# Two-part transformer kernel on one core: a shorter setup ahead of the first block, the rest of the setup as a job of its own, and loads in another order

## The chip, the core and the metric

The kernel runs on one core of a Trainium2 chip. Its engines each have an instruction queue that they work through in order: TensorE (PE, with its weight loads shown as PEld), VectorE (DVE), ScalarE (ACT), GpSimd (POOL) and SyncE (SP), which here only issues DMA transfers. ScalarE and GpSimd issue some transfers too; those of GpSimd stand in the profile as a software queue. The metric is the device time of one execution in microseconds (us); lower is better. The profile's times count from the start of the span.

## The reference

The tokens x are 2 batches of 2048 rows of 256 numbers, all in float32. A vector c of each batch gives six rows of modulation, and two networks follow, the first of 3 layers of linear attention (16 heads), the second of 2 layers of windowed attention. Cut to what matters here:

```python
mod = silu(c) @ wmod                 # 6 rows of 256 per batch: shift, 1 + scale, gate, twice
h = layernorm(x) * (1 + scale_1) + shift_1
for l in range(3):                   # linear attention with exponential features of omega
    q, k, v = h @ Wq[l] + bq[l], h @ Wk[l] + bk[l], h @ Wv[l] + bv[l]
    a = causal_linear_attention(exp_features(q, omega[l]), exp_features(k, omega[l]), v)
    h = layernorm(h + a @ Wo[l] + bo[l]) * ln1_g[l] + ln1_b[l]
    h = layernorm(h + relu(h @ W1[l] + bf1[l]) @ W2[l] + bf2[l]) * ln2_g[l] + ln2_b[l]
x = x + gate_1 * h
h = layernorm(x) * (1 + scale_2) + shift_2
# two layers of windowed attention and a gated MLP on h, then x + gate_2 * (their output)
```

## The kernel before

**Setup.** `vec` holds c and all small parameters as columns, `cst` the identity and masks, `wmod` the modulation weights. A silu of c (`sg`) is multiplied by all six parts of `wmod` in 24 products of two columns each (`pm`, L300), which become `mod`. Parameters that are added or multiplied along the free dimension are wanted as rows, the same in every partition (`brow`, 18 rows: R_G1, R_B1, R_G2, R_B2 for the layers, R_G0, R_B0 for the first norm, R_GE, R_BE for the end). `spread` makes them on the engines: VectorE copies two columns out to 512 wide (`wide`, L279), TensorE turns them in four transposes (`rowtp`, L287), ScalarE copies them into `brow` (L288); nine such rounds. `omt` (L330 to L337) is omega laid out for the heads, from `om_rep`, which GpSimd loads in eight pieces.

**Loads.** SyncE's queue holds, in this order: `vec`, `cst`, one half of `wmod`, the tokens of the first two blocks, the weights of all three layers, the tokens of the third and fourth block. ScalarE issues the other half of `wmod` and the first layer's `Wq`. GpSimd issues `bvb` and `om_rep`.

**Blocks.** The first part works on 16 blocks (b, n) of 256 tokens, n in order and both batches in turn. `favor_block` norms the tokens (`normed`: statistics L354, `dn` L361), turns them (`turned`: `ntp` L371, evicted into `h` L375), makes the residual rows on GpSimd (`scaled`: `res`, L384 and L385, which read `brow`), and runs three layers. A layer (`favor_layer`) is: projections `pq` (L414, evicted by VectorE into `xs` L425, squared by ScalarE L426) and `pv` (L430), features `pu` (L453), running sum `z` (VectorE L475, then GpSimd's copy `zl` L484 and product L485), transposes `tk`, scores `sc` (L500), `su`, denominators `den` (L548, which read `z`), `nd`, output `po` (L602), norm, and the MLP with `pf` (L624), `fr` (L632) and `acc` (L635).

**Order.** `planned` takes the blocks as generators and keeps four of them live; each step says how much TensorE time it takes and how long its result needs, and the block that is ready first goes next. TensorE's queue in the first part is exactly that order. The other engines and SyncE get their order from a list scheduler. At the start all four live blocks are normed and turned before the first `pq`.

**Seam.** The last block stores `hm` to DRAM (L690), the second part loads it as `s` (L724), and the weights `w2` (L198) are loaded about there too. The second part has an order written out by hand, which the change doesn't touch.

Of the kernel before, what the change touches and what calls it, by code (L numbers as in the profile page):

```python
# [39 lines left out]
def block_kernel(ctx: ExitStack, tc: tile.TileContext, t: dict, out: bass.AP):  # L40
# [19 lines left out]
    nc.sync.dma_start(cst, t["consts"])  # L60
# [11 lines left out]
    mhalf = const.tile([P, 16], F32, name="mhalf")  # L72
    nc.gpsimd.memset(mhalf, -0.5)
    mod = const.tile([P, 6, KT, B], F32, name="mod")
    omt = const.tile([P, LA, 2, 4, 2, 8], F32, name="omt")
    bvb = const.tile([P, LA, D], F32, name="bvb")
    nc.gpsimd.dma_start(bvb, t["bv"].partition_broadcast(P))
# [134 lines left out]
    with ExitStack() as c1:  # L212
        wp = c1.enter_context(tc.tile_pool(name="wA", bufs=1))
        psum = c1.enter_context(tc.tile_pool(name="psA", bufs=1, space=PSUM))
        brow = wp.tile([P, NROW, D], F32, name="brow")
        hp = c1.enter_context(tc.tile_pool(name="hA", bufs=3))
        work = c1.enter_context(tc.tile_pool(name="workA", bufs=2))

# [10 lines left out]
        with tc.tile_pool(name="pro", bufs=1) as pro:  # L229
            wmod = pro.tile([P, KT, 6 * D], F32, name="wmod")  # L230
            for kt in range(KT):
                (nc.scalar if kt else nc.sync).dma_start(wmod[:, kt, :], t["wmod"][kt * P : (kt + 1) * P, :])
            early = {b: load_x(b, 0) for b in range(B)}
            om_rep = pro.tile([P, LA, 8], F32, name="om_rep")
            for h in range(8):
                nc.gpsimd.dma_start(om_rep[16 * h : 16 * h + 16], t["omega"].rearrange("l d m -> d l m"))
            W = {}
            for l in range(LA):
                pool = shared if l < 2 else wp
                wa = pool.tile([P, ROOM], F32, tag=f"wa{l}", name=f"wa{l}")  # L240
                wb = pool.tile([P, ROOM], F32, tag=f"wb{l}", name=f"wb{l}")
                for room, at, name, kts, width in (
                    (wa, KT * DFF, "Wq", KT, D),
                    (wa, KT * DFF + KT * D, "Wk", KT, D),
                    (wb, NF * D, "Wv", KT, D),
                    (wb, NF * D + KT * D, "Wo", KT, D),
                    (wa, 0, "W1", KT, DFF),
                    (wb, 0, "W2", NF, D),
                ):
                    w = room[:, at : at + kts * width].rearrange("p (k n) -> p k n", k=kts)  # L250
                    (nc.scalar if (name, l) == ("Wq", 0) else nc.sync).dma_start(
                        w, t[name][l].rearrange("(k p) n -> p k n", p=P)
                    )
                    W[name, l] = w

            cv = vec[:, V_C : V_C + KT * B]
            sg = pro.tile([P, KT * B], F32, name="sg")
            nc.scalar.activation(sg, cv, AF.Exp, scale=-1.0)
            nc.vector.tensor_scalar(sg, sg, 1.0, None, ALU.add)
            nc.vector.reciprocal(sg, sg)  # L260
            nc.vector.tensor_tensor(sg, sg, cv, ALU.mult)

            cols = pro.tile([P, NROW, KT], F32, name="cols")

            def col(i, *parts):
                op = parts[2] if len(parts) > 2 else ALU.add
                if len(parts) == 1:
                    nc.vector.tensor_copy(cols[:, i, :], parts[0])
                else:
                    nc.vector.tensor_tensor(cols[:, i, :], parts[0], parts[1], op)  # L270

            def va(l, name):
                o = V_A + l * VA_N + VA[name]
                return vec[:, o : o + KT]

            def spread(lo, hi):
                for i in range(lo, hi, 2):
                    wide = pro.tile([P, 2 * KT, P], F32, tag="wide", name="wide", bufs=2)
                    nc.vector.tensor_copy(  # L279
                        wide,  # L280
                        cols[:, i : i + 2, :].rearrange("p a k -> p (a k)").unsqueeze(2).to_broadcast(
                            [P, 2 * KT, P]
                        ),
                    )
                    tp = mm_tile("rowtp").rearrange("p (a c) -> p a c", c=P)
                    for k in range(2 * KT):
                        nc.tensor.transpose(tp[:, k, :], wide[:, k, :], ident)  # L287
                    nc.scalar.copy(brow[:, i : i + 2, :].rearrange("p a (k c) -> p (a k) c", c=P), tp)  # L288

            for l in range(LA):  # L290
                col(R_G1 + l, va(l, "g1"))
                col(R_B1 + l, va(l, "b1"), va(l, "bf2"))
            for l in range(LA - 1):
                col(R_G2 + l, va(l, "g2"))
                col(R_B2 + l, va(l, "b2"), va(l + 1, "bo"))
            spread(0, R_G0)
            pm = mm_tile("pm")
            for m in range(6 * KT):
                for kt in range(KT):
                    nc.tensor.matmul(  # L300
                        pm[:, m * B : (m + 1) * B],
                        wmod[:, kt, m * P : (m + 1) * P],
                        sg[:, kt * B : (kt + 1) * B],
                        start=(kt == 0),
                        stop=(kt == KT - 1),
                    )
            nc.vector.tensor_copy(mod.rearrange("p a k b -> p (a k b)"), pm[:, : 6 * KT * B])
            for i in (1, 4):
                nc.vector.tensor_scalar(mod[:, i], mod[:, i], 1.0, None, ALU.add)
            for i in (2, 5):  # L310
                sgn = pro.tile([P, KT, B], F32, name=f"sgn{i}")
                nc.vector.tensor_scalar(sgn, mod[:, i], 0.0, 2.0, ALU.is_ge, ALU.mult)
                nc.vector.tensor_scalar(sgn, sgn, -1.0, None, ALU.add)
                neg = pro.tile([P, KT, B], F32, name=f"neg{i}")
                nc.vector.tensor_scalar(neg, mod[:, i], -1.0, None, ALU.mult)
                nc.vector.tensor_tensor(neg, neg, mod[:, i], ALU.max)
                nc.vector.tensor_scalar(neg, neg, 0.25, None, ALU.max)
                nc.vector.tensor_tensor(mod[:, i], sgn, neg, ALU.mult)
            for b in range(B):
                col(R_G0 + b, mod[:, 1, :, b])  # L320
                col(R_B0 + b, mod[:, 0, :, b], va(0, "bo"))
                col(R_GE + b, va(LA - 1, "g2"), mod[:, 2, :, b], ALU.mult)
                col(R_BE + b, va(LA - 1, "b2"), mod[:, 2, :, b], ALU.mult)
            spread(R_G0, NROW)


            for hf in range(2):
                own, other = slice(64 * hf, 64 * hf + 64), slice(64 - 64 * hf, 128 - 64 * hf)
                for l in range(LA):
                    nc.vector.tensor_tensor(  # L330
                        omt[own, l, hf].rearrange("p h s m -> p (h s) m"),
                        om_rep[own, l, :].unsqueeze(1).to_broadcast([64, 8, 8]),
                        hm2[own, 8 * hf : 8 * hf + 8].unsqueeze(2).to_broadcast([64, 8, 8]),
                        ALU.mult,
                    )
                    nc.vector.tensor_scalar(omt[own, l, hf], omt[own, l, hf], 0.5, None, ALU.mult)
                    nc.vector.tensor_scalar(  # L337
                        omt[other, l, hf].rearrange("p h s m -> p (h s m)"),
                        nhalf[other, 64 - 64 * hf : 128 - 64 * hf],
                        0.25,  # L340
                        None,
                        ALU.mult,
                    )

        rp = c1.enter_context(tc.tile_pool(name="rA", bufs=2))
        fp = c1.enter_context(tc.tile_pool(name="featA", bufs=2))
        sp = c1.enter_context(tc.tile_pool(name="smallA", bufs=2))
# [45 lines left out]
        nc.vector.tensor_reduce(par, hmask.rearrange("p (i q) -> p q i", q=2), AX.X, ALU.add)  # L393
# [5 lines left out]
        turn = [0]  # L399

        def favor_layer(b, n, l, h, hres):
# [45 lines left out]
            yield 5.2, 0.6, "attention"  # L447
            feat = []
# [171 lines left out]
            for f in range(NF + 1):  # L620
                if f < NF:
# [9 lines left out]
                    fr[f] = fp.tile([P, TA], F32, tag="fr", name="fr", bufs=3)  # L631
# [37 lines left out]
        def favor_block(b, n):  # L669
            dn = normed(early.pop(b) if n == 0 else load_x(b, n))  # L670
            yield 0.0, 4.0
            h = hp.tile([P, KT, TA], F32, tag="h", name="h0")
            turned(dn, h, lambda k: mod[:, 1, k, b : b + 1], lambda k: mod[:, 0, k, b : b + 1])
            hres = scaled(dn, R_G0 + b, R_B0 + b)
# [18 lines left out]
        with tc.manual_schedule(engines={mybir.EngineType.PE}):  # L693
            planned([favor_block(b, n) for n in range(S // TA) for b in range(B)], 4)
# [632 lines left out]
```

## Time and profile before

| | us |
|---|---|
| median of 3 runs | 3002.98 (3001.48 to 3004.59) |
| profiled execution | 3000.0 |
| its span | 2998.2 |
| PE busy | 2914.3 (97%) |
| DVE, ACT, POOL busy | 1686.0, 1344.5, 1065.1 |
| first `pq` on TensorE | 46.14 |
| mean granted clock | 0.992 |

The first part ends near 1590, the second takes the rest. The page's busy times are sums over the span; what the start costs is seen only in the stretches and in the chain of waits of the first microseconds.

### The profile page before, as it was taken

How to read it: one execution, taken by the hardware profiler on the slowest of the kernel's cores; microseconds unless marked ns; L12 is line 12 of the kernel's file. 1: busy time of each engine (PE TensorE's matmuls, PEld its weight loads, DVE VectorE, ACT ScalarE, POOL GpSimd, SP SyncE). 2: the span in 40 equal slices, each digit the busy share in tenths (PEclk: the TensorE clock that was granted, in tenths of full speed). 3: DMA queues.
4: the chain of work that ended last, by engine and by line, in shares of the span. 5: the costliest groups of instructions: out<-in, count | busy, mean ns of one | idle time of the engine just before them, and what ended most of it. 6: DMA issues, size and time to landing. Idle time of an engine off the chain costs nothing.

```text
span 2998.2 us, 49213 instructions
## 1 busy us (share of the span) xinstructions
PE 2914.3 (97%) x19356; PEld 2132.3 (71%) x19356; DVE 1686.0 (56%) x4194; ACT 1344.5 (45%) x3269; POOL 1065.1 (36%) x937
## 2 busy tenths in 40 slices
PE   6999999999999999999996999999999999999999
PEld 5888888888888888888873777776444777776444
DVE  5555565555565555655543777774224777775222
ACT  2333343334343334434333676665113766766211
POOL 2222233222332223322233666663002666664000
PEclk9999999999999999999997999999999999999999
DMA  5000010000100000001012000001000000000011
GB/s 184 1 1 1 1 36 22 1 1 1 36 22 1 1 1 29 29 1 43 15 42 77 1 1 1 1 1 58 0 0 10 20 1 1 2 1 8 28 43 35
DMA packets 37399, 57.10 MB, mean 19 GB/s; under 512 B 3720, under 2 KB 28720, under 8 KB 36656
## 3 DMA queue, kind: packets, MB, share of 16 engines
q1 hardware_dynamic: 36288, 52.37, 5.3%
q8 instruction: 153, 2.51, 0.3%
q0 software_dynamic: 464, 0.54, 0.1%
q10 hardware_dynamic: 416, 1.05, 0.1%
q14 instruction: 78, 0.64, 0.1%
HBM read 41.37 MB, written 12.58 MB: 18 GB/s over the span
## 4 chain that ended last, share of the span: by engine, by line
PE 88%; DVE 4%; ACT 3%; POOL 2%; DMA 1%; issue 1%; SPq 1%; DVEq 0%; ACTq 0%; POOLq 0%
PE acc L635 11%; PE pf L624 10%; PE pqkv L790 10%; PE pg L1135 5%; PE pq L414 5%; PE acc L1173 5%; PE pa L1135 4%; PE av L979 4%; PE sim L886 3%; PE ptp L953 3%; PE po L998 3%; PE sc L500 3%; PE nd L572 3%; PE pu L453 3%; PE pv L430 3%; PE po L602 3%
## 5 line engine op out<-in xcount | busy, mean ns | idle before, releaser
L635 PE MATMUL acc<-wb,fr 128*128 128x256 f32 x1536 | 397.3, 381 | 5.4 <-ACT fr L632 5.1
L624 PE MATMUL pf<-h,wa 128*128 128x256 f32 x1536 | 400.2, 384 | 1.1 <-ACT h L375 0.7
L632 ACT ACTIVATE fr<-pf,vec 128x256 f32<-128x256 f32 x384 | 180.6, 471 | 425.8 <-PE pf L624 425.0
L790 PE MATMUL pqkv<-wqkv,s 128*128 128x512 f32 x768 | 358.0, 602 | 8.3 <-issue 8.3
L506 DVE TENSOR_TENSOR att<-sc,cst 128x512 f32<-128x512 f32 x384 | 238.3, 683 | 157.6 <-PE sc L500 157.6
L635 PEld LDWEIGHTS acc<-wb,fr 128*128 128x128 f32 x1536 | 287.8, 190 | 52.0 <-ACT fr L632 8.6
L384 POOL TENSOR_TENSOR res<-dn,brow 128x512 f32<-128x512 f32 x112 | 144.7, 1292 | 485.2 <-DVE dn L361 473.5
L624 PEld LDWEIGHTS pf<-h,wa 128*128 128x128 f32 x1536 | 275.8, 190 | 55.7 <-issue 19.5
L941 POOL TENSOR_TENSOR pm<-pm,sum 128x1024 f32<-128x1024 f32 (+1 forms) x128 | 235.7, 1842 | 178.9 <-DVE sum L936 178.9
L926 ACT ACTIVATE pm<-pm,mx 128x256 f32<-128x256 f32 (+1 forms) x512 | 249.4, 489 | 58.9 <-DVE mx L918 58.7
L790 PEld LDWEIGHTS pqkv<-wqkv,s 128*128 128x128 f32 x768 | 138.0, 193 | 135.9 <-issue 134.0
L832 POOL TENSOR_TENSOR rot<-raw,rsn_wo 128x512 f32<-128x512 f32 x128 | 160.5, 1275 | 183.5 <-ACT raw L813 183.5
L1144 DVE SCALAR_TENSOR_TENSOR ge<-pa,vec,ge 128x512 f32<-128x512 f32 x80 | 60.1, 751 | 281.9 <-PE pa L1135 230.6
L1143 ACT ACTIVATE ge<-pg,vec 128x512 f32<-128x512 f32 x96 | 65.8, 686 | 314.9 <-PE pg L1135 314.9
L426 ACT ACTIVATE xs<-xs 64x512 f32<-64x512 f32 x192 | 120.6, 628 | 152.3 <-DVE xs L425 142.8
L1135 PE MATMUL pg<-s,w 128*128 128x512 f32 (+1 forms) x384 | 182.2, 597 | 0.0
L414 PE MATMUL pq<-h,wa 128*128 128x256 f32 x768 | 175.4, 382 | 0.0
L425 DVE TENSOR_TENSOR xs<-pq,vec 64x512 f32<-64x512 f32 x192 | 132.2, 688 | 76.5 <-PE pq L414 72.7
L1173 PE MATMUL acc<-ge,w 128*128 128x512 f32 (+1 forms) x384 | 168.8, 600 | 0.0
L414 PEld LDWEIGHTS pq<-h,wa 128*128 128x128 f32 x768 | 146.1, 191 | 21.1 <-issue 1.4
L854 POOL TENSOR_TENSOR qk<-qk,rot 128x1024 f32<-128x1024 f32 x64 | 151.5, 2367 | 0.5
L1135 PE MATMUL pa<-s,w 128*128 128x512 f32 x320 | 150.4, 592 | 0.0
(163 smaller groups left out, 5361.8 us busy)
## 6 DMA issues: line engine op xcount, KB each, us to landing
xin<-in_x_dram SPq DMA_DIRECT2D x32, 256.0 KB, 2.8
x<-res SPq DMA_DIRECT2D x16, 256.0 KB, 2.1
h<-hm SPq DMA_DIRECT2D x16, 256.0 KB, 2.4
s<-h SPq DMA_DIRECT2D x16, 256.0 KB, 5.4
xl<-x SPq DMA_DIRECT2D x8, 512.0 KB, 4.2
out_dram<-res SPq DMA_DIRECT2D x8, 512.0 KB, 3.2
w<-in_w_dram SPq DMA_DIRECT2D x6, 640.0 KB, 4.0
wa<-in_W_dram SPq DMA_DIRECT2D x3, 1024.0 KB, 8.9
```

The source lines that it names most:

```text
L414: nc.tensor.matmul(pq[:, g, :], W[wn, l][:, kt, g * P : (g + 1) * P], h[:, kt, :], start=(kt == 0), stop=(kt == KT - 1),)
L506: nc.vector.tensor_tensor(am, scs[i].rearrange("p g q c -> p (g q) c"), caus.unsqueeze(1).to_broadcast([P, 2 * KT, P]), ALU.mult,)
L624: nc.tensor.matmul(pf, W["W1", l][:, kt, f * P : (f + 1) * P], h1[:, kt, :], start=(kt == 0), stop=(kt == KT - 1),)
L632: nc.scalar.activation(fr[f], pf, AF.Relu, bias=v("bf1", f))
L635: nc.tensor.matmul(acc[:, c, :], fr[f - 1][:, c * P : (c + 1) * P], W["W2", l][:, f - 1, :], start=(f == 1 and c == 0), stop=(f == NF), sk ...
L790: nc.tensor.matmul(pq, s[:, kt * TB + c * P : kt * TB + (c + 1) * P], wqkv[:, kt, i * INNER : (i + 1) * INNER], start=(kt == 0), stop=(kt ...
L832: nc.gpsimd.tensor_tensor(rot[:, :, :, lo : lo + 32], got["raw"][:, :, :, hi : hi + 32], rsn[:, ti, :, lo : lo + 32].unsqueeze(2).to_broad ...
L854: nc.gpsimd.tensor_tensor(got["qk"], got["qk"], got["rot"], ALU.add)
L926: nc.scalar.activation(pm[:, hd, :], pm[:, hd, :], AF.Exp, bias=of("mx", hg)[:, hd : hd + 1], accum_out=of("sum", hg)[:, hd : hd + 1],)
L941: nc.gpsimd.tensor_tensor(pm, pm, of("sum", hg).unsqueeze(2).to_broadcast([P, 4, kw]), ALU.mult)
L1135: nc.tensor.matmul(pt[:m, :], w1[:, kt, off : off + m], hb[:, kt * TB : (kt + 1) * TB], start=(kt == 0), stop=(kt == KT - 1),)
L1173: nc.tensor.matmul(acc[m], w2[rs_, f, m * P : (m + 1) * P], g[rs_, :], start=(f == 0), stop=(f == NFH - 1),)
```

## The change

It does five things. (1) A new `first_norm`, in a fixed order on TensorE, VectorE and ScalarE, does what the first block needs: `sg`, the first two of six parts of `mod` (8 products), the first block's norm and turning, the columns, the rows R_G0 and R_B0 and the layer rows, and the first layer's `omt`. (2) The other four parts of `mod`, the other layers' `omt`, the last four rows (R_GE, R_BE) and the loads of the third layer's weights become a job, `rest_of_setup`, which `planned` gets as the second of its live jobs; the fourth block enters when that job is done. (3) `spread` makes rows by DMA: one transpose of the columns, one copy, a store to DRAM, and a load of it into all partitions, both issued by GpSimd. (4) The loads are put in another order: the first third of `wmod` alone on ScalarE, then `Wq` and `Wv`; on SyncE the identity first and the rest of `cst` after the tokens of the first two blocks; the third block's tokens after the first layer's `Wk` and `Wo`; `om_rep` ahead of `bvb`. The third layer's weights take the memory of `wmod` and of the setup's small tiles, so they wait for both. (5) The pools are opened in another order, `fr` moves to another pool, and the first two blocks' `res` rows are made one step later.

By the instruction lists, SyncE's order is now: `vec`, identity, tokens (0,0) and (1,0), rest of `cst`, `Wk`, `Wo`, tokens (0,1), `W1`, rest of `wmod`, `W2`, six weights of layer 1, tokens (1,1), two residual loads, six weights of layer 2. TensorE's: 8 products, 4 transposes, 2 row transposes, `pq` and `pv` of the first block, 8 transposes, `pu`, 4 products, `tk`, `sc`, `su`, 8 products, `sc`, `den`, 4 products, `nd`, `pq` of the second block. GpSimd's: the small loads, the clearing of `vp`, two stores and two loads of rows, four operations on `res`, `zl`, `z`. After the first 200 matmuls TensorE's order is that of before. At the seam, `w2` is now loaded among the loads of `s` and not ahead of the last store of `hm`.

```diff
-    nc.sync.dma_start(cst, t["consts"])
+    nc.sync.dma_start(cst[:, :P], t["consts"][:, :P])
...
+        wmod = wp.tile([P, ROOM], F32, tag="wa2", name="wmod").rearrange("p (k n) -> p k n", k=KT)
+        stage = wp.tile([P, ROOM], F32, tag="wb2", name="stage")
+        nc.scalar.dma_start(wmod[:, :, : 2 * D], wmod_in[:, :, : 2 * D])
+        early = {(b, 0): load_x(b, 0) for b in range(B)}
+        nc.sync.dma_start(cst[:, P:], t["consts"][:, P:])
...
+        load_weights(0, "Wq", "Wk", "Wv", "Wo")
+        early[0, 1] = load_x(0, 1)
+        load_weights(0, "W1")
+        nc.sync.dma_start(wmod[:, :, 2 * D :], wmod_in[:, :, 2 * D :])
+        load_weights(0, "W2")
+        load_weights(1, "Wq", "Wk", "Wv", "Wo", "W1", "W2")
...
+        def spread(lo, hi):
+            n = (hi - lo) * KT
+            tp = mm_tile("rowtp")[:n, :P]
+            nc.tensor.transpose(tp, cols[:, lo:hi, :].rearrange("p a k -> p (a k)"), ident)
+            turned_ = turned_cols.pop()[:n]
+            nc.scalar.copy(turned_, tp)
+            nc.gpsimd.dma_start(rows_out[lo * KT : hi * KT], turned_)
+            nc.gpsimd.dma_start(
+                brow[:, lo:hi, :].rearrange("p a d -> p (a d)"),
+                rows_out[lo * KT : hi * KT].rearrange("a c -> (a c)").partition_broadcast(P),
+            )
...
+        def first_norm(normed, turned):
+            with tc.manual_schedule(
+                engines={getattr(mybir.EngineType, e) for e in ("PE", "DVE", "Activation")}
+            ):
...
+                condition(0, 2, pm)
...
+                dn = normed(early.pop((0, 0)))
+                conditioned(0, 2, pm)
+                turned(dn, h, lambda k: mod[:, 1, k, 0:1], lambda k: mod[:, 0, k, 0:1])
...
+                spread(R_G0, R_GE)
+                spread(0, R_G0)
+                omega_rows(0)
...
+        def rest_of_setup():
+            yield 0.0, 8.0, "mlp"
+            pm = psum.tile([P, NCA * D], F32, tag="acc", name="pm2", bufs=1)
+            for i in range(2, 6):
+                condition(i, i + 1, pm)
+                yield 1.7, 0.0, "mlp"
+            conditioned(2, 6, pm)
...
+            spread(R_GE, NROW)
+            load_weights(2, "Wq", "Wk", "Wv", "Wo", "W1", "W2")
+            yield 0.2, 0.0
...
-                    fr[f] = fp.tile([P, TA], F32, tag="fr", name="fr", bufs=3)
+                    fr[f] = work.tile([P, TA], F32, tag="fr", name="fr", bufs=3)
...
-            planned([favor_block(b, n) for n in range(S // TA) for b in range(B)], 4)
+            blocks = [favor_block(b, n) for n in range(S // TA) for b in range(B)]
+            with tc.issue_after(last_first):
+                planned(blocks[:1] + [rest_of_setup()] + blocks[1:], 4)
```

## The prediction

> **What bounds the kernel now.** First the table of stretches (start:end and length in us, then busy us and instructions of PE, PEld, DVE, ACT and POOL, granted clock, DMA share, GB/s):
>
> ```profile
> 10.00:20.00 10.00, 8.63 (x42) 8.18 (x41) 2.95 (x16) 2.34 (x4) 0.14 (x1) 1.00 1.08 363
> 30.00:40.00 10.00, 2.39 (x12) 1.64 (x10) 3.78 (x8) 3.45 (x8) 6.84 (x7) 0.73 0.96 327
> 40.00:46.00 6.00, 2.26 (x8) 1.42 (x9) 4.73 (x11) 2.02 (x6) 4.32 (x4) 0.50 0.17 45
> 200.00:300.00 100.00, 100.00 (x745) 82.74 (x745) 54.17 (x114) 38.94 (x82) 26.50 (x26) 1.00 0.00 1
> ```
>
> After the start, TensorE is full: 99 us or so in each 100 up to about 1500. Work taken off VectorE, ScalarE or GpSimd there buys nothing; a later or earlier start moves the end one for one. Until 38 us the DMA engines are full at 350 to 400 GB/s, and TensorE does only setup. So I looked at who lets it start. The chain of waits over the first 120 us (start, us, what):
>
> ```profile
> 26.99 12.37 DMA xin<-in_x_dram
> ...
> 43.37 2.03 DVE dn L361 x2
> 45.40 0.04 issue
> 45.44 0.90 PE ntp L371 x3
> 46.34 4.50 PE pq L414 x16
> ...
> 64.48 3.65 PE pq L414 x16
> ```
>
> The first projection (pq) of the first block starts at 46.3. Its own tokens came long before, but TensorE's order puts the transposes of all four live blocks ahead of it, and the last two blocks' tokens are queued on SyncE behind the weights of three layers. Everything in front of 46.3 is start-up; the second block's pq, at 64.48, is my mark: from there TensorE's order is the same in both kernels, but for four transposes and one small transpose.
>
> The timeline of the start gives the prices (start, us, engine, line, what):
>
> ```profile
> 14.18 10.24 PE L300 MATMUL pm<-sg,wmod 128*128 128x2 f32 x48
> ...
> 30.56 0.94 PE L371 MATMUL ntp<-cst,dn 128*128 128x128 f32 x4
> ...
> 32.80 1.25 POOL L384 TENSOR_TENSOR res<-dn,brow 128x512 f32<-128x512 f32 x1
> ...
> 56.93 1.27 POOL L485 TENSOR_TENSOR z<-ft,z 128x512 f32<-128x512 f32 x1
> ...
> 60.68 1.13 PE L548 MATMUL den<-z,cst 128*128 128x256 f32 x4
> ```
>
> and the DMA issues of the first 60 us (KB each, median us to landing):
>
> ```profile
> xin<-in_x_dram SPq DMA_DIRECT2D x7, 256.0 KB, 6.5
> wmod<-in_wmod_dram ACTq DMA_DIRECT2D x1, 768.0 KB, 4.5
> bvb<-in_bv_dram POOLq DMA_DIRECT2D x1, 384.0 KB, 8.0
> om_rep<-in_omega_dram POOLq DMA_DIRECT2D x8, 1.5 KB, 7.6
> ```
>
> **The change, part by part.**
>
> *Start of the first pq.* TensorE now does 8 of the 24 conditioning products, four transposes of the first block, two small transposes, then pq. Two inputs race. (1) The first third of wmod, 512 KB, goes first on ScalarE's queue, where 768 KB landed 4.5 us after 0.77, so about 5.3; sg needs vec (landed at 4.09) and is done by then. 8 products are 16 instructions at 10.24/48 = 0.213: 3.4 us, to 8.7 (at the row's longest single duration, 0.35: 10.9). (2) The first tokens are third on SyncE, behind 57 and 64 KB, issued near 1.7; with the median of 6.5 they land at 8.2 (bounds 2.7 and 10.1 from the same issues: 4.4 and 11.8). From tokens to normed tokens the trace shows 39.38 to 42.55, 3.2 us, less where GpSimd is quiet: 11.2. Then transposes 0.9 and two evictions into h 1.0 (after the mod of path 1): 13.1. The tokens' queue is much shorter than it was, so I take 12.5, bounds 10.5 and 16.5. Wq and Wk are the second transfer of their queue and the sixth; Wq landed at 11.44 even beside both halves of wmod.
>
> *From pq to my mark.* Before, 64.48 - 46.34 = 18.1, with a cold start in it (first pq 4.50 for 16 against 3.65). The same chain follows now, also cold: 18.1.
>
> *Added in that stretch.* VectorE in its fixed order does omega_rows(0) and par before the other blocks' statistics and before the first xs. It waits for eight tiny GpSimd loads; issued from 0.8, 0.6 apart, with 7.6 to land, the last is there at about 12.7. The work behind that up to the first xs (omega's last operations and par 0.6, four statistics at 0.4, one dn pair 0.8, smalls) is some 3.8 us, so xs is at 16.5 instead of 15.5, and one more dn pair lies among the four xs: 2 us, bounds 0.5 and 6. Their eight transposes on TensorE (0.11 each warm, 0.2 cold) fall into that wait.
>
> The other 16 conditioning products, 32 instructions, stand between the steps of the first block. No row shows them warm; transposes halve from 0.21 to 0.11 later in the trace, so 3.4 to 6.8 us. They cover two waits that the chain shows: 0.7 for the exponential before tk, and 1.5 in the second group of sc (2.60 for 16 against 1.08). Without this cover they'd cost all 3.4. Net 1.2 to 4.6; I take 2, nearer the warm end as pq has warmed the clock.
>
> *The rows by DMA.* Out go 36 transposes, 9 evictions (0.59) and 9 wide copies, none of it in front of anything that matters once the start moves. In come, on GpSimd's in-order queue, a small store to DRAM, a load of 512 KB broadcast from it (R_G0 and R_B0), and a second pair of 1.3 MB. Behind them on that queue: four res operations (the second and third blocks' scaled rows), which wait for the 512 KB; behind these zl and z of the first block; and for z waits den on TensorE, with all of its order behind. Price: eviction of the rows done at 13.0; store lands after 5.6 to 7.6 (om_rep), say 6.5: 19.5; broadcast 8.0 (bvb, 384 KB; by size 10.7): 27.5; four res of 1.27: 32.6; zl and z 1.5: 34.1. den is due at 12.5 + 14.4 (60.75 - 46.34) + 2 (VectorE) + 0.4 (the products ahead of it, less what they cover) = 29.3. A wait of 5, bounds 0 (both DMAs at the 4.3 that the 32 KB broadcast of k_scale takes near 1496, with the DMA engines idle) and 8 (7.6 and 10.7). This is the wait that takes the place of the old one. The 1.3 MB are used only after the first block's po, past 45. bvb now stands behind the eight tiny loads: issued near 8.5, landed by 16.5, used near 19. The rest of the constants lands before omega's loads do.
>
> The Trainium skill speaks here: "DMA: Bandwidth & Descriptors", section "Anatomy of one DMA — SWDGE (gpsimd) path", puts such a DMA at 2.0 us plus bytes over 436 GB/s, an estimate of 3.2 us for the 512 KB. By that z would be in time, the wait nothing and the gain 5 us more; this trace shows 8.0 for a smaller one, so the trace goes into the sum. A long wait at den has a second price: the granted clock stood at 0.50 from about 36 to 48, after TensorE had run dry, and the pq begun in that state took 0.85 more; so a wait of that kind adds about a microsecond. The rule for it stands in "TensorE: Matmul & The Clock Gate", Part 1: a window of some 3.4 us without work puts the array back to half clock. By the rule alone even my 5 us would cost that microsecond; I leave it in the range.
>
> *Loads moved.* The third block's tokens now pass W1, wmod's rest and two layers' weights: some 3 MB at 365 GB/s lie ahead of them, so they land before 15 and are used at 17. The fourth block's tokens follow layer 1's weights, some 9 MB at 365 GB/s, 28 us, used after 45. Layer 2's weights wait on SyncE for the rest job and its last row store, until about 45; only later residual tokens queue behind. Their first use was at 264: no cost. W1 and W2 of layer 0 land before 20 and are used after 45.
>
> *Later.* The fourth block's transposes and the last row transpose come after the mark: 0.6 more. At the seam to the second part, the last store of hm no longer shares the DMA engines with w2 (4.1 us there, median 2.4): 1 less, as w2 now stands among the loads of s.
>
> **Sum.** Mark: 12.5 + 18.1 + 2 + 2 + 5 = 39.6 against 64.5, 24.9 gained; less 0.6, plus 1: 25.3. The profiled execution (span 2998.2, 3000.0 in all) would go to 2972.9 and 2974.7. The median of the runs before is 2.98 above the profiled one; I forecast 3002.98 - 25.3 = 2977.7.
>
> **Rivals.**
> - *The rows come later than priced* (store and broadcast each half as slow again, behind layer 1's weights: 9.75 and 16 us): den waits 16 instead of 5, a microsecond for the clock: 2990. For it: the DMA engines are full till 28. Against: no GpSimd DMA of this trace took over 8.0. Chance 0.12.
> - *Everything early*: start at 10.5, no wait at den, VectorE 0.5: 34 gained, 2969. For it: the first tokens are alone on SyncE. 0.12.
> - *Slower*: the pools are laid out anew, and fr moves to another pool, so the operands of pf and acc lie elsewhere in SBUF. If that slowed their 3072 matmuls (381 to 384 ns), each 8.2 ns would eat 25.3 us; from 10.2 ns each the kernel is slower by over 6. Nothing in the trace shows a cost of place. 0.04.
> - *No change*: the start is hidden after all, some other load then holding the first layers. The DMA share of 0.00 to 0.01 from 56 on speaks against it. 0.02.
> - The forecast: 0.70, with its own range 2972 to 2985.
>
> A measurement tells about 0.2%, 6 us, from no change. Range: best ends together (2, 1.5, 0.8 and 5 us better) 2968; start 4, VectorE 4, products 2.6 later and den 3 more would be 2991, not likely all at once: 2968 to 2990. Faster 0.94, same 0.02, slower 0.04.
>
> **What would show it.** In the profile after: pq first at 12 to 13; xs near 16.5; POOL's first res waiting for a DMA into brow until about 27; den waiting for POOL's z about 5 us near 30; the mark near 39.6; from there the same spacings as before. A mark above 52, or pf and acc above 390 ns, would prove me wrong.

## The result

The changed kernel takes 2979.76 us (median of 6 runs, 2977.55 to 2982.33), the kernel before 3002.26 (median of 6, 2999.26 to 3004.59). The ratio is 0.9925, 95% interval 0.9912 to 0.9937: 22.5 us less, where 25.3 was forecast. The profiled execution after (2982.33, span 2980.5) is the slowest of its six, the one before (3000.0) near the lowest of its own, so the two traces differ by only 17.7.

### The profile page after: what moved, and what is told of

Same layout as the page of the kernel before. It is cut to its first block, busy times and chain, and to the rows that moved or that the text cites. A ratio compares the mean times of both kernels' runs of the same rounds, so it can differ in the third digit from the quotient of the medians.

```text
span 2980.5 us, 49140 instructions
## 1 busy us (share of the span) xinstructions
PE 2909.9 (98%) x19323; PEld 2128.4 (71%) x19323; DVE 1681.2 (56%) x4186; ACT 1339.6 (45%) x3263; POOL 1067.1 (36%) x942
## 4 chain that ended last, share of the span: by engine, by line
PE 89%; DVE 4%; ACT 3%; POOL 2%; issue 1%; DMA 1%; ACTq 0%; POOLq 0%; DVEq 0%; SPq 0%
PE acc L698 11%; PE pf L687 10%; PE pqkv L860 10%; PE pg L1205 5%; PE pq L475 5%; PE acc L1243 5%; PE pa L1205 4%; PE av L1049 4%; PE sim L956 3%; PE ptp L1023 3%; PE po L1068 3%; PE nd L635 3%; PE sc L563 3%; PE pu L516 3%; PE po L665 3%; PE pv L491 3%
```

## The profile after

The table of stretches of the changed kernel, columns as before (start:end, length, busy us and instructions of PE, PEld, DVE, ACT and POOL, granted clock, DMA share, GB/s):

```profile
10.00:20.00 10.00, 9.18 (x43) 7.23 (x42) 8.54 (x32) 5.76 (x15) 2.16 (x4) 1.00 1.05 384
30.00:40.00 10.00, 8.24 (x83) 6.88 (x84) 2.25 (x20) 1.32 (x2) 4.19 (x4) 0.58 0.83 243
200.00:300.00 100.00, 100.00 (x800) 82.30 (x799) 53.28 (x115) 37.34 (x79) 23.18 (x23) 1.00 0.00 1
```

TensorE now works from 10 us on, and what it does at 200 is as before. The 1.00 of the first row says nothing up to 14.4, where this trace's clock records begin (in the trace before they begin at 31.3): the first pq takes 5.23 for 16, the second 3.72. But the second row has a granted clock of 0.58 with TensorE busy 82% of the time: much of that "busy" runs at half speed. The chain of waits of the changed kernel (start, us, what) says what came before that:

```profile
12.79 4.25 issue
17.05 7.53 DMA brow<-rows_out
24.73 2.50 POOL res L444 x2
...
30.49 1.23 POOL z L548
31.76 2.07 PE den L611 x4
33.83 1.50 PE pm L316 x8
...
39.36 3.65 PE pq L475 x16
...
66.08 3.65 PE pq L475 x16
```

The rows' store ("issue", since the chain doesn't see into it), the broadcast load, GpSimd's res, z, and den behind it: the wait that the prediction named. The mark, the second block's pq, stands at 39.3 (64.4 before). The DMA issues of its first 60 us (KB each, median us to landing):

```profile
xin<-in_x_dram SPq DMA_DIRECT2D x7, 256.0 KB, 6.2
...
brow<-rows_out POOLq DMA_DIRECT2D x2, 512.0 KB, 7.0
...
wmod<-in_wmod_dram ACTq DMA_DIRECT2D x1, 512.0 KB, 3.9
...
om_rep<-in_omega_dram POOLq DMA_DIRECT2D x8, 1.5 KB, 5.3
```

The pq starts on TensorE's timeline are the ruler for all that follows, each from one profiled execution, beside the medians (us):

| kernel | 1st pq | 2nd | 3rd | 4th | median (runs) |
|---|---|---|---|---|---|
| before | 46.14 | 64.41 | 87.41 | 113.17 | 3002.26 (6) |
| changed | 11.35 | 39.29 | 66.01 | 91.78 | 2979.76 (6) |
| loads_only | 42.64 | 61.70 | 84.70 | 110.47 | 3001.21 (10) |
| late_third | 11.29 | 61.45 | 87.01 | 112.78 | 2998.56 (10) |
| late_res | 11.87 | 38.16 | 68.08 | 93.85 | 2981.31 (4) |
| fourth | 11.48 | 39.71 | 66.43 | 93.28 | 2979.60 (4) |
| norm_late | 11.28 | 39.97 | 62.98 | 93.58 | 2979.55 (5) |
| rows_here | 12.39 | 43.94 | 70.65 | 96.42 | 2987.04 (5) |
| rows_norm | 12.09 | 42.41 | 66.09 | 96.41 | 2985.55 (5) |
| fill | 11.25 | 38.38 | 63.42 | 89.19 | 2978.12 (4) |
| best1 | 11.11 | 37.22 | 60.70 | 91.02 | 2978.90 (4) |
| rows_late | 12.29 | 33.07 | 62.46 | 88.23 | 2975.03 (4) |
| all_three | 12.36 | 33.15 | 56.16 | 85.08 | 2974.24 (4) |

Before minus changed is 34.8 at the first pq, 25.1 at the second, 21.4 at the third, and then stays within 0.1 of 21.4 up to the 47th. So there are two losses to explain: 9.7 between the first and second pq (most of it foreseen), and 3.7 between the second and third (0.6 foreseen). Where each kernel's clock was at 0.50 is part of these figures, and that can differ from one execution to the next (last section).

## The experiments: which part carries the gain

My theory was that the order carries most of it, and that the third block's tokens must come early for that. The rivals were the loads alone, and the order alone.

**loads_only**: the kernel before, with only the loads moved.

```diff
+                if l == 1:
+                    early[0, 1] = load_x(0, 1)
+                if l == 2:
+                    early[1, 1] = load_x(1, 1)
```

> The kernel before, with only its loads in another order: the third block's tokens right after layer 0's weights, the fourth's ahead of layer 2's weights (one more buffer for tokens). Theory 'order' (the gain comes from what TensorE's queue puts ahead of the first pq; loads alone can take off only their own part): all rows are still made first, to 31 us, and the transposes of all four blocks still stand ahead of pq, so the first pq starts near 35 to 37 instead of 46.1, and the run is 9 to 11 us faster than before, 2991 to 2994. Rival 'loads' (the third block's tokens alone are what counted): about the whole gain, 20 us or more, near 2980.

Ratio 0.9997 (0.9988 to 1.0007): no change. The first pq comes 3.5 earlier, not 9 to 11: the old setup keeps VectorE until 31, and the norms of four blocks then follow one another, the last two with 1.6 of wait each for ScalarE's part (TensorE's last transposes wait until 41.6). The gain is down to 2.7 at the next pq.

**late_third**: the changed kernel, with the third block's tokens behind layer 1's weights.

```diff
-        early[0, 1] = load_x(0, 1)
         load_weights(0, "W1")
...
         load_weights(1, "Wq", "Wk", "Wv", "Wo", "W1", "W2")
+        early[0, 1] = load_x(0, 1)
```

> The changed kernel, with the third block's tokens moved back behind layer 1's weights. Theory 'order': they land near 28, their norm ends near 31, and TensorE's queue has their transposes ahead of the first block's pu, which so starts near 32 instead of 19.3; den then no longer waits for z (4.1 us now), so the second block's pq starts at 45 to 48 instead of 39.3 and the run is 6 to 9 us slower than the changed kernel, 2986 to 2989. Rival 'early start is enough' (the pq of the first block at 11 us decides, later waits are covered): within 2 us of the changed kernel, 2980.

2998.56, ratio 0.9983 (0.9973 to 0.9992). Far more was lost than the 6 to 9 us expected: of 22.5 only 3.4 is left (its own runs of the kernel before: 3001.98). The tokens land at 34.2, and TensorE's in-order queue stands before their transposes. Its timeline in this kernel (start, us, engine, line, what; in brackets the idle time ahead and what ended it):

```profile
36.39 1.13 PE L431 MATMUL ntp<-cst,dn 128*128 128x128 f32 x4 [17.52 <-DVE dn L421]
37.45 3.68 PE L516 MATMUL pu<-xs,omt 128*64 128x256 f32 x16
...
61.45 2.73 PE L475 MATMUL pq<-h,wa 128*128 128x256 f32 x9
```

and its stretches (columns as above):

```profile
56.00:60.00 4.00, 4.00 (x48) 3.24 (x51) 1.59 (x18) 0.59 (x1) 0.00 (x0) 0.50 0.53 155
...
64.00:68.00 4.00, 4.00 (x20) 3.51 (x19) 3.22 (x6) 2.51 (x4) 0.00 (x0) 1.00 0.00 1
```

The wait accounts for 17.5. After it TensorE is busy without a gap, yet the clock stays at 0.50 for 26 us, to 62.5, just after the dense pq of the second block has begun: pu takes 3.68 where 1.95 is its time at full clock. Neither of the two works alone: the order needs the third block's tokens early, and early tokens need the order. The other moves among the loads (`wmod`, `cst`, `Wv`) were not tried by themselves.

## The experiments: the wait for z and the clock

**late_res**: the changed kernel, with res of the first three blocks made just before use, so that z does not stand behind four of them.

```diff
-            if callable(hres):
-                hres = hres()
             feat = []
...
+            if callable(hres):
+                hres = hres()
             s = work.tile([P, NCA, D], F32, tag="s", name="s1")
...
-            if n > 0:
+            if n > 1 or (b, n) == (1, 1):
                 hres = hres()
```

> The changed kernel, with the res rows of the first three blocks made one step before their use, so that in GpSimd's queue only one operation on res, not four, stands ahead of the first z. Theory 'order': z ends near 28 to 29 instead of 31.7, den follows, and with less of a wait the clock falls less; the second block's pq starts 2.5 to 4 us earlier (35 to 37) and the run is 2.5 to 4 faster than the changed kernel, about 2976.5. Rival 'rows' (the wait is for the broadcast itself, whatever stands behind it): no change, 2980. Rival 'clock' (the microseconds near den come from the half clock alone): the wait goes, but den, products and nd stay at 6.5 us together, and under 2 us are gained.

TensorE's timeline in this kernel:

```profile
30.50 2.00 PE L609 MATMUL den<-z,cst 128*128 128x256 f32 x4 [1.34 <-POOL z L546]
...
38.16 3.72 PE L475 MATMUL pq<-h,wa 128*128 128x256 f32 x16
...
55.03 0.47 PE L431 MATMUL ntp<-cst,dn 128*128 128x128 f32 x1 [3.86 <-DVE dn L421]
```

den's wait falls from 4.1 to 1.3, but the mark comes only 1.1 earlier, for two reasons. The clock falls after the short wait too: from den to pq it is 7.66 here and 7.53 in the changed kernel, which is what the rival 'clock' said. And in this execution TensorE reaches den 1.5 later, since the first pq begins 0.5 later and takes 6.22, not 5.23, with the clock up only at 16.95 (14.4 there). best1 below has the same edit without that delay, and its mark comes 2.1 earlier, at 37.22. Behind the mark 3.2 more is lost: VectorE now does att ahead of the fourth block's dn, and TensorE's transposes wait 3.9 for that. 2981.31: nothing gained.

**fill**: the changed kernel, with fourteen products of den's shape in the wait.

```diff
+            if old is None and (b, n, l) == (0, 0, 0):
+                for r in range(14):
+                    nc.tensor.matmul(den[:, r % KT, :], nhalf, qf[:, r % KT, :], start=True, stop=True)
             for g in range(KT):
                 nc.tensor.matmul(den[:, g, :], nhalf, z[:, g, :], start=True, stop=True)
```

> The changed kernel with fourteen products of the den shape (128 partitions x 256 columns, about 0.28 each, 3.9 together) written into den's PSUM ahead of the first den, so that TensorE works through its wait for GpSimd's z; the true den overwrites them. Theory (the wait of 4.1 costs its length, and beyond it about 3 for the granted clock of 0.50 to 0.71 that follows): z still ends at 31.7, den starts at 31.7 to 32.2, the granted clock holds over 0.9 between 28 and 40, den takes 1.1 to 1.2 in place of 2.07, and the second pq comes at 36 to 37 in place of 39.3: 2976 to 2977.5. Rival (the clock falls for the narrow products ahead, the sixteen conditioning products of two columns, whatever stands in the wait): den takes 2.0, second pq at 39 to 40, 2979 to 2981.

TensorE's timeline in this kernel:

```profile
27.83 6.31 PE L612 MATMUL den<-ft,cst 128*128 128x256 f32 x28
33.98 1.03 PE L614 MATMUL den<-z,cst 128*128 128x256 f32 x4
...
38.38 3.72 PE L475 MATMUL pq<-h,wa 128*128 128x256 f32 x16
```

I had the filler at 3.9; each product is two instructions, and it took 6.3. So den starts 2.2 later than in the changed kernel, and still the mark comes 0.9 earlier. The granted clock is 1.00 from 15 on. From den to pq it is 4.40 here and 7.53 in the changed kernel: **the clock's price for that wait is 3.1 us**, shown apart from the wait itself. The rival (it falls whatever stands there) is out. The mark missed its own forecast of 36 to 37 by the longer filler, and the time, 2978.12, is not clear of the changed kernel's.

**rows_here**: the changed kernel, with the four rows R_G0 and R_B0 made by the old transposes, so that res no longer waits for their broadcast. (The layer rows' store and the issue of their load still stand ahead of res in GpSimd's queue; res starts at 19.37, not near 17.)

```diff
-                spread(R_G0, R_GE)
+                spread_here(R_G0, R_GE)
```

> The changed kernel with the four rows that res and the layer's end need at first made on the engines again: two VectorE copies of 128x512, eight 128x128 transposes on TensorE and two ScalarE copies, in place of a store to DRAM and a 512 KB broadcast load that lands at 24.6. Theory (the den product's wait of 4.1 for GpSimd's z, behind the res that wait for that load, and the clock of 0.50 to 0.71 after it, are the price of the DMA): the first pq comes at 12.5 to 14 in place of 11.35 (two copies near 0.6 each and ten small products near 0.15 stand ahead of it), res start near 17, den waits under 0.5, no slice of the granted clock between 26 and 40 is under 0.9, the second block's pq comes at 34.5 to 36.5 in place of 39.3, and the time is 2975 to 2977. Rival (the clock falls in any case, since TensorE idles between its first products): den does not wait, the clock still falls under 0.8 and the second block's pq comes at 37.5 to 39, time 2978 to 2979.5. Rival (the products ahead of the first pq cost as much as the wait): second block's pq at 39 or later.

This went the wrong way: mark at 43.94, 2987.04, ratio 0.9946 (0.9933 to 0.9958). den waits no more, but VectorE does. Its timeline in this kernel:

```profile
18.76 0.18 DVE L359 TENSOR_SCALAR omt<-omt 64x64 f32<-64x64 f32 x1
18.95 5.43 DVE L360 TENSOR_SCALAR omt<-cst 64x64 f32<-64x64 f32 x1
24.30 0.22 DVE L353 TENSOR_TENSOR omt<-om_rep,cst 64x64 f32<-64x64 f32 x1
```

and GpSimd's:

```profile
19.37 2.52 POOL L460 TENSOR_TENSOR res<-dn,brow 128x512 f32<-128x512 f32 x2
21.83 2.48 POOL L461 TENSOR_TENSOR res<-res,brow 128x512 f32<-128x512 f32 x2
```

A VectorE instruction of 0.19 lasts 5.43, and ends with the last of GpSimd's four res (it began 0.42 ahead of the first, while GpSimd issued that load). qe is late by that, TensorE's sc waits 4.6, and the clock, at 0.50 from then on, is back only at about 43. In the changed kernel the slow broadcast put these res (24.7 to 29.7) where VectorE had only att and sum to do, which read PSUM and keep their 2.48 and 0.68. Making the rows sooner moved the collision onto the path.

**rows_late**: rows made on the engines, and res made just before use (the edits of rows_here and late_res together).

> The first rows made on the engines, and res of the first three blocks made only where they are used. With the rows on the engines but res early, the second pq came at 43.94: VectorE's 64x64 feature weights, 0.19 each elsewhere, held one instruction for 5.43 while GpSimd made four res in one stretch of 5.0, and qe, sc and the clock followed. Theory (that stretch is what costs, not the rows' way): no feature-weight instruction on VectorE over 1, qe ends by 23.5, the clock holds, second pq at 34 to 37, and the time 2976 to 2979 with the 3.7 after it left as in the changed kernel. Rival (the engines' copies and transposes ahead of the first pq are the cost): second pq at 40 or later, 2981 to 2985.

2975.03, ratio 0.9907 (0.9890 to 0.9923), 28.0 below its own kernel before. The mark comes at 33.07, the earliest of all, with no wait in front of den and a clock of 1.00. TensorE's timeline in this kernel:

```profile
28.57 1.13 PE L625 MATMUL den<-z,cst 128*128 128x256 f32 x4
...
33.07 3.72 PE L491 MATMUL pq<-h,wa 128*128 128x256 f32 x16
```

VectorE's feature weights take 0.17 to 0.22 each. So making the rows on the engines costs little in itself; the stretch of res does. And with res late in both, rows on the engines (33.07) beat rows by DMA (late_res 38.16, best1 37.22) at the mark. 2.7 of the 6.2 us is lost again on the way to the third pq (29.4 instead of 26.7).

## The experiments: the loss behind the mark

**fourth**: the changed kernel, with the fourth block's transposes planned later, its norm where it was.

```diff
-                yield 0.0, 4.0
+                yield 0.0, 16.0 if (b, n) == (1, 1) else 4.0
```

> The changed kernel, with the fourth block's first transposes put 12 us later in the plan (its delay after the norm 16 instead of 4), so that they come after the third block's pq and no longer ahead of the first block's first pf. Theory 'order': the distance from the second to the third block's pq, 26.7 us in the changed kernel against 23.0 before, goes back to about 23, and the run is 3 to 4 us faster, about 2976. Rival 'VectorE' (VectorE's extra work there, and not the order on TensorE, delays the chain): the distance stays above 25.5 and less than 1.5 us is gained.

Still 26.72 from second to third pq, 2979.60. The wait only moved, to pf, 2.7 of it. The trace names no releaser; VectorE's att, which frees pf's PSUM, stands behind the fourth block's norm, and its first instruction ends at 55.3, just ahead of pf at 55.46. So it isn't TensorE's order, but VectorE's.

**norm_late**: the changed kernel, with the norm itself planned 20 units later.

```diff
+                if (b, n) == (1, 1):
+                    yield 0.0, 20.0
                 dn = normed(early.pop((b, n)) if (b, n) in early else load_x(b, n))
```

> The changed kernel with the fourth block's norm itself planned 20 units later, so that VectorE does the second block's first two groups of att (L569), the z and the norm of s ahead of the fourth block's statistics and dn, and GpSimd's res of the fourth block comes later too. In the changed kernel 26.72 us lie between the second and the third pq, 23.0 in the kernel before. Theory (VectorE's order: statistics 0.7, aggregates 0.2 and dn 1.6 of the fourth block stand ahead of att, and the z scan beside GpSimd's res takes 2.3 in place of 1.3, together 3.6, which TensorE's pf waits for through a PSUM slot): the distance falls to 23 to 24, the wait of the first pf from 2.7 to under 0.7, every later mark is 2.5 to 3.7 earlier, time 2976 to 2977.5. Rival (the distance is TensorE's own load of products, and the wait only moves to the next one): the distance stays over 26, time 2979 to 2981. Second rival (the norm now collides with the third block's att one pq later): the distance falls and the next one grows by as much, time as the changed kernel.

The distance is 23.01, as before the change (23.00). But the next is 30.60 (25.77 in the changed kernel), and on TensorE's timeline there:

```profile
80.46 2.00 PE L687 MATMUL pf<-h,wa 128*128 128x256 f32 x4 [2.18 <-DVE att L569]
```

pf waits 2.2 for att, and the clock falls again. The second rival was right: the norm is a cost that moves. 2979.55.

**rows_norm** and **best1** join norm_late with rows_here and with late_res, **all_three** with both.

> Both edits at once: the first rows made on the engines and the fourth block's norm planned later. Theory (two separate prices, 3 to 4 us each, that add): second pq at 34.5 to 36.5, third pq 23 to 24 behind it, time 2971.5 to 2974.5. Rival (what is gained early is lost again before the second layer's weights or at another wait for VectorE): the marks after the third pq give back over half, time 2975 to 2978.

> Two earlier edits together: res of the first three blocks made just before they are used, and the fourth block's norm planned 20 units later. Theory (the norm of the fourth block costs TensorE 4 to 5 us wherever it stands in the order, so only the shorter wait for z is gained): second pq at 38.2, third 23 behind it at 61.2, fourth at 91 to 92.5 as in the changed kernel, 2978 to 2980. Rival (without GpSimd's res beside it the norm is half as long on VectorE, 0.8 in place of 1.6, and hides): fourth pq at 87 to 89, 2974 to 2977.

> Rows made on the engines, res of the first three blocks made where they are used, and the fourth block's norm planned 20 units later. Theory (each edit keeps what it gave: second pq at 33 as with the first two; third pq 23.5 behind it, as with the norm late; 30.3 from third to fourth, since the norm's cost only moves): fourth pq at 86 to 88 in place of 88.2 and 91.8, time 2972 to 2975. Rival (with the first half earlier the weights of the second layer or another load come last): the distance from second to third pq is over 25, time 2975 to 2978.

rows_norm: 2985.55, the mark late as in rows_here, since the 5 us collision is there again (an omt of 5.22). best1: 2978.90, fourth pq at 91.02 as its theory had it. all_three: 2974.24 (2972.80 to 2974.95), ratio 0.9908 (0.9892 to 0.9925), fourth pq at 85.08. Against their own runs of the kernel before, rows_late gains 28.0 and all_three 26.9, the changed kernel 22.5. No run of the changed kernel stood beside them on their chip, and the intervals overlap, so I say no more than that both are probably some 5 us better.

## Why the prediction was right, and where only by a sum

**First pq**: 12.5 forecast, 11.35 measured. The first third of wmod landed at 4.83 (5.3 forecast), its 16 instructions took 3.54 (3.4). The first xs was at 14.89, not 16.5.

**den's wait**: 5 forecast, 4.09 measured. The price was built right, piece by piece: store 5.3 (6.5), broadcast 7.53 (8.0), four res 5.0 (5.1). (Its upper bound of 8 is 8.6 by its own terms.) One detail was wrong: the res belong to the third and the first block, not to the second and third. The Trainium skill, "DMA: Bandwidth & Descriptors", section "Anatomy of one DMA — SWDGE (gpsimd) path", would have given an estimate of 3.2 for the broadcast; the run shows 7.53 beside full DMA engines, so the row decides.

**The products**: 2 forecast. Behind den they cost 0.7 at full clock (den to pq 4.40 in fill, 3.73 before), where 1.6 of the 2 was meant. TensorE was ready for den at 27.7, not 29.3, mostly by the earlier start.

**The clock**: "about a microsecond", and left out of the sum. It was 3.1 (fill). This is a term that was mis-sized, and it didn't show, because den began 2.5 earlier than forecast (31.76 for 34.3): the mark came out as 39.3 for 39.6 by errors of opposite sign, which is luck.

**After the mark**: 0.6 forecast, 3.7 measured, and this is the step that failed. "The fourth block's transposes and the last row transpose come after the mark: 0.6 more" counts what TensorE issues and not what it waits for: the fourth block's norm on VectorE (statistics 0.7, aggregates 0.2, dn 1.6), with a z scan stretched from 1.27 to 2.27 beside GpSimd's res of the first block. On VectorE's timeline of the changed kernel:

```profile
50.54 2.27 DVE L538 TENSOR_TENSOR_SCAN z<-ft,zero 128x256 f32<-128x256 f32 x2
52.73 1.61 DVE L421 TENSOR_SCALAR dn<-xin,mv,rs 128x256 f32<-128x256 f32 x2
54.26 2.47 DVE L569 TENSOR_TENSOR att<-sc,cst 128x512 f32<-128x512 f32 x4
```

and on TensorE's:

```profile
54.16 0.78 PE L431 MATMUL ntp<-cst,dn 128*128 128x128 f32 x4 [1.87 <-DVE dn L421]
55.04 3.40 PE L687 MATMUL pf<-h,wa 128*128 128x256 f32 x8
58.24 1.32 PE L698 MATMUL acc<-wb,fr 128*128 128x256 f32 x4
```

1.9 of wait, and then eight pf in 3.40 (2.06 at full clock, twice 1.03) and four acc in 1.32 (1.03): 1.6 for the clock. fill shows the two apart, since in its execution the clock held behind the same wait:

```profile
53.26 0.78 PE L431 MATMUL ntp<-cst,dn 128*128 128x128 f32 x4 [1.87 <-DVE dn L421]
54.14 1.96 PE L690 MATMUL pf<-h,wa 128*128 128x256 f32 x8
55.94 1.03 PE L701 MATMUL acc<-wb,fr 128*128 128x256 f32 x4
```

Its third pq comes 25.04 behind the second: 2.0 of the 3.7 is the wait, 1.7 the clock. In the kernel before, that norm was done from 39.4 to 45.4, ahead of the first pq, where TensorE had only these transposes to do.

**Seam**: 1 forecast; the gain grows there from 17.95 to 19.93, so 2, of which the last store of hm gives 1.7 (2.43 in place of 4.10). Just ahead of it 3.5 is lost, between 1482 and 1492, which I had not foreseen: GpSimd's 32 KB load of k_scale took 6.0 in place of 4.3, with a cooler clock after it. Such a loss stands in the traces of the other kernels too, from 1.2 (fill) to 3.5. Why it differs is left open. Behind the seam the gain falls again, from 20.1 to the 17.7 of the two spans, 1.6 of it near 2032, where the changed kernel's granted clock is at 0.50 for 3.4 us and fill's stays at 1.00.

**Rivals**: the rows were not late; "everything early" was near on the start (10.5) but not on the absence of a wait; no cost of place showed. On the page after:

```profile
L698 PE MATMUL acc<-wb,fr 128*128 128x256 f32 x1536 | 398.5, 382 | 7.0 <-ACT fr L695 5.1
L687 PE MATMUL pf<-h,wa 128*128 128x256 f32 x1536 | 402.4, 385 | 0.6 <-DVE att L569 0.3
```

382 and 385 ns in the mean, against 381 and 384 before.

## What to carry to other kernels

A start that is brought forward brings forward all that used to hide in it: list what every engine did in the old gap, and find each piece a new cover, not only those on the bounding engine. A wait on TensorE costs its length and, often, a cold stretch behind it; dense products put into the wait show the second apart from the first. Before a GpSimd job is made earlier, look at what VectorE does then.

## What the runs showed of the hardware

- **The clock changes on a grid of 3.41 us.** In the changed kernel the granted clock fell at 28.10, came back at 38.34, fell at 55.40 and came back at 58.82: 10.24, 17.06 and 3.42 apart, 3, 5 and 1 times 3.41. In every trace of this case the distances between its changes are such multiples (before: 34.67 and 48.32, 4 times), and the grid lies elsewhere in each execution. So that the clock fell only 0.4 us after TensorE stopped at 27.7, and behind waits of 1.3 (late_res, best1), doesn't make these waits a threshold: the change came at the grid's next instant, and what a wait costs beyond its length depends on where it falls on the grid. The same wait of 1.87 left the clock at 0.50 behind it in the changed kernel and at 1.00 in fill.
- **A busy row is not a warm clock.** After the wait for z it took 6.5 us of work to come back, in late_third 26 us, both times mostly of small or partly filled products (two columns, 32 rows); when it fell again at 55.4, dense pf brought it back in 3.4. The Trainium skill, "TensorE: Matmul & The Clock Gate", Part 1, gives one window of about 3.4 us, idle or busy, for either turn. The grid and the dense products agree with that; late_third's 26 us without a gap at half clock show that "busy" in a profile is not what decides. That the small products were the reason, there and where a short wait was enough, was not tried.
- **GpSimd and VectorE block each other.** 0.19 became 5.43 beside res (5.22 in rows_norm; in rows_late, with res moved away, all stay at 0.22 or less), z scans went from 1.27 to 2.27 (1.27 again in norm_late, where res comes after the scan), dn from 0.7 to 1.6 a pair, while att, which reads PSUM, kept its 2.48. The Trainium skill, "GPSIMD Engine Reference", section "1. Specifications", says that the two share their way into SBUF and contend in some VectorE instructions; that one small instruction can be held for a whole stretch of GpSimd work is what these runs add.
